# Turning all adjacency rows once, beside layer 0 of the first element, in a four-layer graph kernel

## The chip, the cores and the metric

The kernel runs on one core of a Trainium2 chip. The metric is the device time of one execution in microseconds (us), and the median of several runs is quoted. The engines are called by the names of the profile: PE is the matrix engine (TensorE), PEld its loading of weights, DVE the vector engine, ACT the scalar engine, POOL GpSimd, and SP the engine whose queue issues this kernel's transfers. SBUF is the on-chip working memory, PSUM the memory that PE writes to, DRAM the chip's main memory.

## The reference

There are B = 16 graphs, called elements here, of N = 1024 nodes with D = 64 features each, and an adjacency matrix of 1024 x 1024 zeros and ones per element. Four residual layers follow each other. Before each of them the features are normalised over their 64 values and cut at zero.

```python
# layer 0: thinned adjacency, weighted quantiles over each node's neighbours, two-layer network
h = jnp.maximum(_layernorm(x, axis=-1), 0.0)
x = x + _L0_gnn_ref(h, adj, nodemask, L0_gnn_W1, L0_gnn_b1, L0_gnn_W2, L0_gnn_b2)
# layer 1
h = jnp.maximum(_layernorm(x, axis=-1), 0.0)
A = adj + jnp.eye(N)                                   # _L1_gnn_ref(h, adj)
x = x + jnp.einsum('bij,bjd->bid', A, h) / jnp.sum(A, axis=2, keepdims=True)   # nan -> 0
# layer 2: attention with eight heads, adjacency as a bias on the scores
h = jnp.maximum(_layernorm(x, axis=-1), 0.0)
gamma = jnp.exp(h @ W_gamma.T + b_gamma)
attn = softmax(gamma[..., 0] * q @ k.T * D ** -0.5 + gamma[..., 1] * adj)
x = x + (attn @ v) @ W_proj.T + b_proj
# layer 3
h = jnp.maximum(_layernorm(x, axis=-1), 0.0)
x = x + jnp.einsum('bij,bjo->bio', adj, h @ weight) + bias
```

Layers 1 and 3 both multiply the adjacency matrix by a 1024 x 64 matrix. The matrix engine contracts over partitions, so it wants the columns of the adjacency matrix on the partitions, and the rows must be turned (transposed) first.

## The kernel before

Each element is worked in blocks of 128 nodes: C = 8 blocks, P = 128 partitions, and NH = 2 halves of 512 columns.

**Layer 0** is the largest part. `picks()` (L779) walks through 16 x 8 x 2 x 6 steps of element, feature group, half and quantile. One step is called a comparison: three large DVE operations (`le`, `wa`, `wb` at L819, L821, L823), sums on PE (`prep` and `val`, L842), copies of these on ACT (`wi`, `vs`), a bit test on DVE (L857), a sum on PE (L862) and a product on DVE (L869). An element has 96 of them. `group()` (L713) makes the tables for these comparisons on PE and ACT. `background()` (L967) runs beside them and prepares the next element: it ranks the features of a pair of elements (`ranks`, DVE and transfers of masks `md`) and thins the next adjacency matrix (`dilate`, L470, which reads adjacency rows too). `stages()` (L1016) prepares the next element's neighbour masks near the end of an element, and `leave()` (L1052) runs the small network at its end and gives the element to `done`.

**Layers 1 to 3** of an element are a generator, `rest()` (L1253). In layer 1 (L1089) each block of 128 rows is loaded (`adj_rows`, L465), passed over by ACT in place with an accumulator that gives the row's sum (L1097), turned by `chunk_cols` (L450: eight PE transposes into two PSUM tiles and two ACT copies into `aT`), stored turned to DRAM (`adjT_d`, L1099), and used in `weighted` (L1073: matrix products, a copy, a small product). Layer 3 (L1229) loads the turned blocks back (L1244) and uses `weighted` again. Layer 2 (L1112) loads the rows once for each of four pairs of heads, forms scores on PE, adds the bias and takes the row's extremum on DVE (L1199), exponentiates on ACT, turns the result by `chunk_cols` (`eT`), and multiplies by the values (L1213).

**What sets the order.** The two generators are woven together by a credit, at the end of the program:

```python
    two, due = layers(), 0.0
    for r in picks():
        due += r
        while due > 0.0:
            due -= next(two) or due
```

Each comparison credits 0.42 units. The `yield` values in the layers are their prices: 0.5 + 8 x 0.3 + 0.2 for layer 1, 0.7 + 4 x (0.5 + 8 x 1.0) for layer 2, 0.5 + 8 x 0.3 for layer 3. While the layers wait for an element that layer 0 has not finished, they yield None and the credit is dropped. When all comparisons are done, `alone` is set and the rest of the layers runs by itself with more buffers. Within this program order a scheduler fixes the order of the instructions on each engine when the kernel is built, and every engine then works through its own in that order.

**Buffers and queues.** Adjacency rows use a ring of three buffers (tag `adj`) for layers 1 and 2 and for thinning. Turned blocks use a ring of two (tag `bt`), shared by `aT` and layer 2's `eT`; once `alone` is set, `chunk_cols` has six buffers of another tag. All transfers are issued on SP's queue, one after the other; a transfer that waits for its buffer or its data holds those behind it.

Of the kernel before, what the change touches and what calls it, by code (L numbers as in the profile page):

```python
# [8 lines left out]
F32 = mybir.dt.float32  # L9
# [6 lines left out]
AF = mybir.ActivationFunctionType  # L16
OP = mybir.AluOpType
# [4 lines left out]
P = 128  # L22
# [16 lines left out]
def tile_preln_adj_stack(  # L39
# [30 lines left out]
    nc = tc.nc  # L70
    B, N, D = x.shape
    C = N // P
# [7 lines left out]
    dram = ctx.enter_context(tc.tile_pool(name="dram", bufs=2, space=DRAM))  # L80
# [6 lines left out]
    def tb(name, shape, dt):  # L87
        return sb.tile(list(shape), dt, tag="tb", bufs=6, name=name)
# [5 lines left out]
    def b2_(name, shape=(P, 512), dt=F32):  # L94
        return sb.tile(list(shape), dt, tag="b2", bufs=6, name=name)
# [16 lines left out]
    def pb(name, shape=(P, 512), dt=F32):  # L112
        if alone and name != "pcols":
            return pa(name, shape, dt)
        return ps.tile(list(shape), dt, tag="pb", bufs=2, name=name)

    def small(name, shape, dt=F32, bufs=3):
        return sb.tile(list(shape), dt, tag="s_" + name, bufs=bufs, name=name)
# [271 lines left out]
    sb = ctx.enter_context(tc.tile_pool(name="sb", bufs=1))  # L390
# [11 lines left out]
    def bc(ap, shape):  # L402
        return ap.to_broadcast(list(shape))

    def act(out_, in_, func=AF.Copy, **kw):
        nc.scalar.activation(out_, in_, func, **kw)  # L406

    def adjoining(made):

        first = next(made)  # L410
        with tc.issue_after(first.ins), tc.high_priority():
            for _ in made:
                pass


    def norm_relu(xr, h, t2):

        sh = [P, C, D]
        mean = small("mean", [P, C])
        nc.vector.tensor_reduce(mean, xr, AX.X, OP.add)  # L420
        nc.vector.tensor_scalar(mean, mean, 1.0 / D, None, op0=OP.mult)
        d = t2("d", (P, C, D))
        nc.vector.tensor_tensor(d, xr, bc(mean[:, :, None], sh), OP.subtract)
        sq = t2("sq", (P, C, D))
        act(sq, d, AF.Square)
        ve = small("ve", [P, C])
        nc.vector.tensor_reduce(ve, sq, AX.X, OP.add)
        nc.vector.tensor_scalar(ve, ve, 1.0 / D, EPS, op0=OP.mult, op1=OP.add)
        sd = small("sd", [P, C])
        act(sd, ve, AF.Sqrt)  # L430
        r = small("r", [P, C])
        nc.vector.reciprocal(r, sd)

        e = small("e", [P, C])
        nc.vector.tensor_tensor(e, r, r, OP.mult)
        nc.vector.tensor_tensor(e, e, ve, OP.mult)
        nc.vector.tensor_scalar(e, e, -0.5, 1.5, op0=OP.mult, op1=OP.add)
        nc.vector.tensor_tensor(r, r, e, OP.mult)
        nc.vector.scalar_tensor_tensor(h, d, 0.0, bc(r[:, :, None], sh), op0=OP.max, op1=OP.mult)

    def to_cols(h, hT, rows):

        n = h.shape[2]
        for s in range(NH):
            pt = pb("pt", (n, 4, P))
            for c in range(4):
                nc.tensor.transpose(pt[:, c, :], h[:, 4 * s + c, :], identf)
            nc.scalar.copy(hT[rows, s * 512 : (s + 1) * 512], pt[rows].rearrange("d c p -> d (c p)"))

    def chunk_cols(ad, name):  # L450

        aT = (
            tb(name, (P, C, P), F32) if alone
            else sb.tile([P, C, P], F32, tag="bt", bufs=2, name=name)
        )
        for s in range(2):
            pt = pb("pcols", (P, 4, P))
            adjoining(
                nc.tensor.transpose(pt[:, c, :], ad[:, (4 * s + c) * P : (4 * s + c + 1) * P], identf)  # L459
                for c in range(4)  # L460
            )
            nc.scalar.copy(aT[:, 4 * s : 4 * s + 4, :], pt)  # L462
        return aT

    def adj_rows(b, c):  # L465
        ad = sb.tile([P, N], F32, tag="adj", bufs=3, name="ad")
        nc.sync.dma_start(ad, adj[b, c * P : (c + 1) * P, :])
        return ad
# [604 lines left out]
    def weighted(aT, h):  # L1073

        two = pb("two", (P, P))
        adjoining(
            nc.tensor.matmul(  # L1077
                two[j % 2 * D : j % 2 * D + D, :], h[:, j, :], aT[:, j, :], start=j < 2,
                stop=j >= C - 2, tile_position=(0, j % 2 * D), skip_group_check=True,
            )  # L1080
            for j in range(C)
        )
        part = small("aoT", [P, P], bufs=2)
        nc.scalar.copy(part, two)
        po = pb("po", (P, D))
        nc.tensor.matmul(po, part, ident2, start=True, stop=True)
        return po

    def layer1(b, xr, adjT_d):  # L1089
        h = b2_("h1", (P, C, D))  # L1090
        norm_relu(xr, h, b2_)
        yield 0.5
        o = sb.tile([P, C, D], F32, tag="po", bufs=1, name="o1")
        rc = small("rc1", [P, C], bufs=2)
        for i in range(C):
            ad = adj_rows(b, i)
            act(ad, ad, AF.Copy, accum_out=rc[:, i : i + 1])  # L1097
            aT = chunk_cols(ad, "aT1")
            nc.sync.dma_start(adjT_d[i], aT)  # L1099
            nc.scalar.copy(o[:, i, :], weighted(aT, h))  # L1100
            yield 0.3
        nc.vector.tensor_scalar(rc, rc, 1.0, None, op0=OP.add)
        nc.vector.reciprocal(rc, rc)
        nc.vector.tensor_tensor(o, o, h, OP.add)
        nc.vector.tensor_tensor(o, o, bc(rc[:, :, None], [P, C, D]), OP.mult)
        bad = b2_("bad", (P, C, D), I32)
        nc.vector.tensor_tensor(bad, o, o, OP.not_equal)
        nc.vector.copy_predicated(o, bad, bc(none[:, :, None], [P, C, D]))
        nc.vector.tensor_tensor(xr, xr, o, OP.add)
        yield 0.2  # L1110
# [115 lines left out]
                yield 0.3  # L1226
        residual(*late.pop())

    def layer3(b, xr, adjT_d):  # L1229
        h = b2_("h3", (P, C, D))  # L1230
        norm_relu(xr, h, b2_)
        hT = sb.tile([P, N], F32, tag="hT2", bufs=1, name="h3T")
        to_cols(h, hT, slice(0, D))
        ph = pb("ph3", (P, C, D))
        for j in range(C):
            nc.tensor.matmul(ph[:, j, :], hT[:D, j * P : (j + 1) * P], w3, start=True, stop=True)
        hid = b2_("hid3", (P, C, D))
        nc.scalar.copy(hid, ph)
        nc.vector.tensor_tensor(xr, xr, bc(b3r[:, None, :], [P, C, D]), OP.add)
        yield 0.5  # L1240
        o = sb.tile([P, C, D], F32, tag="po", bufs=1, name="o3")
        for i in range(C):
            aT = sb.tile([P, C, P], F32, tag="bt", bufs=2, name="aT3")
            nc.sync.dma_start(aT, adjT_d[i])  # L1244
            nc.scalar.copy(o[:, i, :], weighted(aT, hid))
            yield 0.3
        nc.vector.tensor_tensor(xr, xr, o, OP.add)
        nc.sync.dma_start(out[b].rearrange("(c p) d -> p c d", p=P), xr)
# [3 lines left out]

    def rest(b):  # L1253
        xr = done.pop(b)
        adjT_d = dram.tile([C, P, C, P], F32, name="adjT_d")
        yield from layer1(b, xr, adjT_d)
        yield from layer2(b, xr)
        yield from layer3(b, xr, adjT_d)

    def layers():  # L1260
        for b in range(B):
            while b not in done:
                yield None
            yield from rest(b)
# [5 lines that stand above are left out]
# [39 lines left out]
```

## Time and profile before

| | |
|---|---|
| median of 3 runs | 12679.28 us (12668.32 to 12680.48) |
| the profiled execution's own time | 12671.61 us |
| its span, first to last instruction | 12669.8 us |
| PE, DVE, ACT busy | 11341.0, 11563.5, 9468.7 us |
| granted PE clock, mean | 0.981 |
| bytes read and written in DRAM | 616.27 MB, 206.57 MB |
| transfers on SP's queue, share of the 16 DMA engines | 19.7% |

A busy time is the union of the recorded instructions of an engine. PE's records are pipelined, so it can be called busy without being at its peak. A window gives the same numbers for a stretch of the span. In a group's name, `out<-in` are the program's tile names with their digits left out, so that `c` stands for both `c0` and `c1`. A wait is put down to the instruction that ended it.

Most of the span is periodic. The first comparison starts at 346.2 us and the ninety-seventh, the first of element 1, at 979.7 us. From there on each element takes between 739 and 784 us up to element 13, 721 us for element 14 and 675 us for element 15, for which no further element has to be prepared. The last comparison starts at 12237.0 us.

### The profile page before, as it was taken

What the parts mean: (1) busy time and instruction counts of PE and PEld (TensorE: products, weight loads), DVE (VectorE), ACT (ScalarE), POOL (GpSimd) and SP (SyncE); (2) the same over time, 40 slices, a digit from 0 to 9 for tenths busy, and PEclk for the clock granted to TensorE, in tenths of its full rate; (3) what the DMA queues carried; (4) which work ended last, traced back from release to release, by engine and by line L of the source; (5) the groups of instructions that cost most, each with busy time, mean ns of one, the idle gap of its engine ahead of it and who ended that gap; (6) DMA issues with size and microseconds to landing.
All of it is one profiled execution on the core that took longest, in us unless ns stands there. A gap on an engine that the chain in (4) does not pass through costs nothing. (4 is left out here: it accounts for less than half of the span.)

```text
span 12669.8 us, 216982 instructions
## 1 busy us (share of the span) xinstructions
PE 11341.0 (90%) x84671; PEld 5347.0 (42%) x84673; DVE 11563.5 (91%) x19682; ACT 9468.7 (75%) x17028; POOL 1.3 (0%) x10
## 2 busy tenths in 40 slices
PE   0779999989899998999989999899998999999998
PEld 0224444444444444444444444444444444444445
DVE  8999989999898998999999999999999999988863
ACT  0557777778777777777877788777887877888866
POOL 0000000000000000000000000000000000000000
PEclk9999999999999999999999999999999999999999
DMA  3012121221212212121121212212121121302121
GB/s 105 28 41 70 52 87 53 66 78 59 83 54 72 73 55 83 53 91 57 57 83 53 94 56 67 76 61 85 56 90 52 64 84 56 99 30 66 34 72 60
DMA packets 503175, 841.07 MB, mean 66 GB/s; under 512 B 238720, under 2 KB 273664, under 8 KB 502144
## 3 DMA queue, kind: packets, MB, share of 16 engines
q1 hardware_dynamic: 502144, 827.20, 19.7%
q8 instruction: 662, 10.85, 0.3%
q14 instruction: 369, 3.02, 0.1%
HBM read 616.27 MB, written 206.57 MB: 65 GB/s over the span
## 5 line engine op out<-in xcount | busy, mean ns | idle before, releaser
L821 DVE TENSOR_TENSOR wa<-le,c 128x2048 f16<-128x2048 f16 x1536 | 1868.2, 1216 | 206.8 <-PE prep L842 173.6
L735 PE MATMUL px<-valid,cw 128*128 128x512 fp8e4 x8192 | 1979.9, 382 | 0.0
L819 DVE TENSOR_TENSOR le<-cum,krow 128x2048 f16<-128x2048 int16 x1536 | 1863.4, 1213 | 12.3 <-PE val L842 10.2
L823 DVE TENSOR_TENSOR wb<-le,c 128x2048 f16<-128x2048 f16 x1536 | 1866.8, 1215 | 1.2 <-PE prep L842 1.2
L406 ACT ACTIVATE c<-px,shifts 128x512 f16<-128x512 f32 x2048 | 1415.3, 698 | 278.9 <-PE px L756 139.0
L406 ACT ACTIVATE s<-s,nm 128x1024 f32<-128x1024 f32 x1024 | 1172.6, 1148 | 188.2 <-DVE nm L1199 184.6
L735 PEld LDWEIGHTS <-cw 128*128 128x128 f16 x8192 | 802.5, 98 | 1113.6 <-issue 231.2
L459 PE MATMUL pcols<-identf,s 128*128 128x128 f32 x8192 | 1168.9, 280 | 94.6 <-ACT eT L462 44.3
L1190 PE MATMUL sp<-kT,qT 64*128 64x512 f32 x4096 | 1166.2, 643 | 61.9 <-DVE nm L1199 59.4
L849 ACT COPY wi<-prep 128x512 f32<-128x512 f32 x1536 | 910.7, 593 | 373.1 <-PE prep L842 301.9
L842 PE MATMUL val<-le,tab 128*32 128x512 f16 x12288 | 1154.6, 386 | 18.1 <-DVE vs L869 7.3
L406 ACT ACTIVATE high<-px,shifts 128x512 f16<-128x512 f32 x1024 | 710.6, 694 | 602.5 <-PE px L735 599.3
L459 PEld LDWEIGHTS pcols<-identf,s 128*128 128x128 f32 x8192 | 900.2, 141 | 617.0 <-ACT eT L462 273.7
L869 DVE SCALAR_TENSOR_TENSOR vs<-pz,vs 128x512 f32<-128x512 f32 x1536 | 1046.6, 681 | 113.7 <-PE pz L862 110.7
L462 ACT COPY eT<-pcols 128x512 f32<-128x512 f32 x2048 | 1134.4, 604 | 20.8 <-PE pcols L459 18.1
L1213 PE MATMUL ao<-eT,v 128*64 128x128 f32 x16384 | 1080.2, 276 | 17.9 <-ACT eT L462 14.0
L406 ACT ACTIVATE vs<-val 128x512 f32<-128x512 f32 x1536 | 938.0, 611 | 161.5 <-PE val L842 108.2
L1213 PEld LDWEIGHTS ao<-eT,v 128*64 128x64 f32 x16384 | 907.5, 137 | 294.6 <-ACT eT L462 135.0
L1199 DVE CUSTOM_DVE_ANT_0 s<-sp,ad,nm 128x512 f32<-128x512 f32 x1024 | 725.9, 744 | 137.8 <-PE sp L1190 137.3
L857 DVE TENSOR_SCALAR bit<-wi,to 128x512 int32<-128x512 int32 x1536 | 826.3, 538 | 2.2 <-ACT cw L406 2.2
L842 PE MATMUL prep<-wb,sel_w 128*32 128x512 f16 x6144 | 650.4, 394 | 189.2 <-DVE wb L823 183.1
L1199 DVE CUSTOM_DVE_ANT_0 s<-sp,ad 128x512 f32<-128x512 f32 x1024 | 681.2, 682 | 128.8 <-PE sp L1190 104.8
(271 smaller groups left out, 18238.8 us busy)
## 6 DMA issues: line engine op xcount, KB each, us to landing
ad<-in_adj_dram SPq DMA_DIRECT2D x768, 512.0 KB
adjT_d<-aT SPq DMA_DIRECT2D x128, 512.0 KB
aT<-adjT_d SPq DMA_DIRECT2D x128, 512.0 KB
md<-sm SPq DMA_DIRECT2D x216, 256.0 KB
sb<-md SPq DMA_DIRECT2D x216, 256.0 KB
rem_d<-rem SPq DMA_DIRECT2D x128, 256.0 KB
left_d<-nb SPq DMA_DIRECT2D x128, 256.0 KB
lr<-left_d SPq DMA_DIRECT2D x256, 128.0 KB
```

The source lines that it names most:

```text
L406: nc.scalar.activation(out_, in_, func, **kw)
L459: nc.tensor.transpose(pt[:, c, :], ad[:, (4 * s + c) * P : (4 * s + c + 1) * P], identf)
L462: nc.scalar.copy(aT[:, 4 * s : 4 * s + 4, :], pt)
L735: yield nc.tensor.matmul(px[pp], w[:, j, :], valid[:, j, :], start=False, stop=j == C - 1, skip_group_check=True,)
L819: nc.vector.tensor_tensor(le, cum, bc(el.krow[q][:, None, hs], [P, 4, 512]), OP.is_lt)
L821: nc.vector.tensor_tensor(wa, le, c0, OP.mult)
L823: last = nc.vector.tensor_tensor(wb, le, c1, OP.mult)
L842: yield nc.tensor.matmul(dst[32 * pp : 32 * pp + 32, :], w[pp], r[pp], start=i == 2, stop=i in (1, 3), tile_position=(0, 32 * pp), skip_gr ...
L869: nc.vector.scalar_tensor_tensor(vs, pz, 80.0, vs, op0=OP.is_equal, op1=OP.mult)
L1190: nc.tensor.matmul(sps[e], qT[e * D : (e + 1) * D, i * P : (i + 1) * P], kT[e * D : (e + 1) * D, hs], start=True, stop=True,)
L1199: nc.vector.tensor_tensor_reduce(ss[e][:, hs], sps[e], ad[:, hs], -1.0, 3.0e38 if t == 0 else nms[e], op0=OP.add, op1=OP.min, accum_out=nm,)
L1213: nc.tensor.matmul(ao[e * D : (e + 1) * D, :], v[:, j, e * D : (e + 1) * D], eTs[e][:, j, :], start=j == 0, stop=j == C - 1, tile_position ...
```

## The change

A new generator, `turned()`, runs ahead of all layers. It goes through the 128 row blocks of all 16 elements: it loads a block, passes over it on ACT with the accumulator (the sums go to one tile, `degree`), turns it and stores it to one of sixteen DRAM tensors, `adjT`, one for each element. Each block has the price 0.3, so the 128 of them cost 38.4 units of the 40.32 that element 0's comparisons credit. Layer 1 no longer loads, sums or turns rows: it loads the turned blocks by `turned_rows()`, as layer 3 did and does, and each of its blocks has the price 0.25 in place of 0.3. The row sums come from `degree`.

```diff
-    def layer1(b, xr, adjT_d):
+    def turned():
+        for b in range(B):
+            for i in range(C):
+                ad = adj_rows(b, i)
+                act(ad, ad, AF.Copy, accum_out=degree[:, b * C + i : b * C + i + 1])
+                nc.sync.dma_start(adjT[b][i], chunk_cols(ad, "aT1"))
+                yield 0.3
+
+    def turned_rows(b, i, name):
+        aT = sb.tile([P, C, P], F32, tag="bt", bufs=2, name=name)
+        nc.sync.dma_start(aT, adjT[b][i])
+        return aT
+
+    def layer1(b, xr):
         h = b2_("h1", (P, C, D))
         norm_relu(xr, h, b2_)
         yield 0.5
         o = sb.tile([P, C, D], F32, tag="po", bufs=1, name="o1")
+        for i in range(C):
+            nc.scalar.copy(o[:, i, :], weighted(turned_rows(b, i, "aT1"), h))
+            yield 0.25
         rc = small("rc1", [P, C], bufs=2)
-        for i in range(C):
-            ad = adj_rows(b, i)
-            act(ad, ad, AF.Copy, accum_out=rc[:, i : i + 1])
-            aT = chunk_cols(ad, "aT1")
-            nc.sync.dma_start(adjT_d[i], aT)
-            nc.scalar.copy(o[:, i, :], weighted(aT, h))
-            yield 0.3
-        nc.vector.tensor_scalar(rc, rc, 1.0, None, op0=OP.add)
+        nc.vector.tensor_scalar(rc, degree[:, b * C : (b + 1) * C], 1.0, None, op0=OP.add)
...
         for i in range(C):
-            aT = sb.tile([P, C, P], F32, tag="bt", bufs=2, name="aT3")
-            nc.sync.dma_start(aT, adjT_d[i])
-            nc.scalar.copy(o[:, i, :], weighted(aT, hid))
+            nc.scalar.copy(o[:, i, :], weighted(turned_rows(b, i, "aT3"), hid))
             yield 0.3
...
-        adjT_d = dram.tile([C, P, C, P], F32, name="adjT_d")
...
+    adjT = [dram.tile([C, P, C, P], F32, name=f"adjT{b}", bufs=1) for b in range(B)]
+    degree = sb.tile([P, B * C], F32, tag="degree", bufs=1, name="degree")
 
     def layers():
+        yield from turned()
         for b in range(B):
             while b not in done:
                 yield None
             yield from rest(b)
```

More of the change, by code (lines that the diff above doesn't have):

```diff
@@ L1227, in layer2, with layer3 @@
         residual(*late.pop())
-    def layer3(b, xr, adjT_d):
+    def layer3(b, xr):
         h = b2_("h3", (P, C, D))
@@ L1254, in rest @@
         xr = done.pop(b)
-        adjT_d = dram.tile([C, P, C, P], F32, name="adjT_d")
-        yield from layer1(b, xr, adjT_d)
+        yield from layer1(b, xr)
         yield from layer2(b, xr)
-        yield from layer3(b, xr, adjT_d)
+        yield from layer3(b, xr)
+    adjT = [dram.tile([C, P, C, P], F32, name=f"adjT{b}", bufs=1) for b in range(B)]
+    degree = sb.tile([P, B * C], F32, tag="degree", bufs=1, name="degree")
     def layers():
+        yield from turned()
         for b in range(B):
```

## The prediction

> **What bounds the kernel now.** I read the page first: the engines' totals, then the costliest groups. The chain that ended last covers only the final part of the span (13% of it), so after that I worked from windows.
>
> ```profile
> PE 11341.0 (90%) x84671; PEld 5347.0 (42%) x84673; DVE 11563.5 (91%) x19682; ACT 9468.7 (75%) x17028; POOL 1.3 (0%) x10
> ```
>
> Two engines are near full and ACT has a quarter free. The order of the comparisons (L819, 96 to an element) cuts the span into stages: start-up to 346 us, element 0's comparisons to 980, fifteen mixed stretches (layer 0 of one element beside layers 1 to 3 of the element before), and a tail from 12237, the last comparison. The windows (columns: stretch, length, busy of PE, PEld, DVE, ACT, POOL, granted clock, DMA share, GB/s) for element 0, an early, a late and the last mixed stretch:
>
> ```profile
> 346.10:979.70 633.60, 504.42 (x2882) 154.78 (x2882) 615.00 (x844) 367.23 (x605) 0.00 (x0) 0.94 0.11 36
> 4806.90:5590.90 784.00, 720.47 (x5301) 335.17 (x5300) 735.56 (x1202) 593.98 (x1067) 0.00 (x0) 0.98 0.20 67
> 9339.20:10099.40 760.20, 698.01 (x5294) 330.70 (x5293) 736.77 (x1205) 590.06 (x1065) 0.00 (x0) 0.99 0.21 71
> 11562.10:12237.00 674.90, 650.48 (x5043) 307.73 (x5041) 575.18 (x876) 541.20 (x990) 0.00 (x0) 1.00 0.14 46
> ```
>
> Element 0 is bound by DVE (615 of 634) and ACT idles 266 us: this is where the change puts work. Stretches 1 to 13 are bound by DVE with PE close behind; the last two by PE (650 of 675). The same work took 784 us early and 760 late. The boundary, 12 comparisons before a new element to 24 after, holds the difference: elements 2, 6, 12 and 13:
>
> ```profile
> 1636.70:1951.90 315.20, 282.07 (x2139) 136.98 (x2140) 273.64 (x450) 237.67 (x441) 0.00 (x0) 0.96 0.26 83
> 4709.00:5027.00 318.00, 283.42 (x2133) 137.42 (x2133) 276.61 (x455) 236.76 (x440) 0.00 (x0) 0.96 0.26 82
> 9238.20:9540.20 302.00, 277.74 (x2139) 135.14 (x2137) 275.96 (x455) 242.79 (x449) 0.00 (x0) 0.98 0.27 87
> 10002.90:10288.70 285.80, 268.40 (x2095) 131.84 (x2091) 262.57 (x445) 230.30 (x429) 0.00 (x0) 0.99 0.29 93
> ```
>
> DVE idles 41 us at an early boundary and 23 to 26 at a late one; elsewhere it idles about 1 us in 12 comparisons. What drifts between early and late is the lag of the layers: one element's layers cost 40.7 units (3.1 + 34.7 + 2.9) and its 96 comparisons credit 96 x 0.42 = 40.32, so the layers fall 0.38 units further back each time, and layer 3 and layer 1 slide off the boundary. Layer 1 itself, from first to last weighted sum of element 4:
>
> ```profile
> 4119.60:4158.90 39.30, 37.55 (x337) 20.83 (x333) 35.63 (x54) 30.21 (x64) 0.00 (x0) 1.00 0.59 198
> ```
>
> PE is at 96% here and DVE still at 91%. The tail, with layer 1 of element 15 in its second line, layer 2 in the third, layer 3 in the last:
>
> ```profile
> 12237.00:12268.00 31.00, 29.03 (x240) 16.45 (x240) 21.43 (x50) 24.90 (x47) 0.00 (x0) 1.00 0.20 70
> 12268.00:12345.00 77.00, 58.99 (x478) 47.73 (x474) 14.96 (x37) 31.22 (x81) 0.00 (x0) 0.73 0.52 181
> 12345.00:12637.00 292.00, 257.34 (x1992) 169.34 (x1992) 111.87 (x315) 207.72 (x388) 0.00 (x0) 0.94 0.16 53
> 12637.00:12669.80 32.80, 24.50 (x161) 20.09 (x160) 0.69 (x1) 4.98 (x18) 0.00 (x0) 0.50 0.31 104
> ```
>
> **What the Trainium skill says.** "Perfetto Trace Analysis", section "Identifying the Most-Contended Engine", warns that matmul occupancy misleads because matmuls are pipelined. The trace agrees: one L735 matmul shows 382 ns, yet 8192 of them cover 1979.9 us, 242 ns each. So I price PE by cover. The same page, "Optimizing Scalar/DVE Operations", says that a profiled latency holds a write acknowledgement that overlaps with the next instruction. Again it agrees: back-to-back L462 copies show 587 ns but start 477 ns apart. "DMA: Bandwidth & Descriptors", section "Anatomy of one DMA", gives about 2.0 us fixed plus bytes over 436 GB/s, an estimate of 3.2 us for 512 KB; in the chain of waits such loads show 3.9 to 5.5 us, and the trace decides.
>
> **The change part by part.**
>
> *One turned row* costs PE eight transposes. The pcols group covers 1168.9 us with 8192, so 8 take 1.14 us. It costs ACT one 1024-wide activation (starts 0.96 apart), its accumulator read (0.09) and two copies (0.48 each): 2.0 us. SP issues a load and a store (0.33 us each). DVE does nothing.
>
> *Element 0.* The built kernel issues the 128 rows evenly: the first five ahead of the first comparison's copies (three of their activations in start-up, where ACT is idle), the last at 89 to 91. ACT gets 123 x 2.0 = 246 us; layer 0 there sums to 345 by starts, so 591 of 634, 93%. PE gets 128 x 1.14 = 146 beside a busy time of 504 that is inflated by pipelining. SP gets 256 issues, 84 us, and DMA another 128 MB, 212 GB/s; layer 1 of the kernel before ran at 188 to 204 GB/s. Lower end 0: everything fits under DVE. Upper end +97: layer 1 turned its rows 5.7 us apart (seven intervals in about 40 us) while 128 in 634 us asks for 4.95, and 128 x 5.7 = 730. Each of the three adjacency buffers is held through a load (4 us), ACT's queue and the transposes, and thinning borrows one of them. Behind a store that waits for its copies SP holds the ranking's mask stores, the thinned rows and the eight-row results of layer 0; DVE and the next element's layer 0 wait for those, with two to six buffers of slack. In the last 24 comparisons ACT's own sums (68 and 76 us) meet stretches of 74 and 68, so it binds there. I take **+40**.
>
> *Layer 1, elements 0 to 14.* Removed per element: 9.1 us of PE, 16 of ACT, one load and one store per row. Added: one load per row from DRAM, through two buffers. Layer 3 reads the same way already: SP waited 265.7 us in all for those buffers, but PE waited only 11.7 us in 16 cases for the landed rows. Behind the waiting load SP holds the next adjacency loads of layer 2 and layer 0's results. The load and store saved give that time back, so I price it at 0 (cover: layer 0's work; without it, 8 landings of about 4 us per element). Each layer 1 is also 0.4 units cheaper (8 x 0.05): layers cost 40.3 against 40.32 credited, so the lag is gone. Every stretch then carries 0.38 units more; the groups L459, L1190 and L1213 cover 3415 us for 512 units, 6.7 us a unit, so 2.5 us of PE and 1 of DVE.
>
> The two effects meet at the boundary. No lag means early boundaries throughout: 41 us of idle DVE instead of the mean 33, +8. Against that, layer 1 was bound by PE and by its transpose-copy-sum chain: 9 us (PE alone) to 25 (PE and ACT in series) go. I take 13. Net -5 in each of 13 stretches: **-65**, from -220 (25 and no loss) to +100 (no relief). Stretches 14 and 15 are bound by PE: 9.1 - 2.5 less, but a worse boundary; **-6** together.
>
> *Tail.* 15 x 0.38 = 5.7 units of element 14 stood behind the last comparison; they move forward. Layer 1 of element 15 then runs alone: about 8 us of norm, eight rows 3.0 us apart (as layer 3's: 12641.35, 12644.36, 12647.38), five DVE operations of 0.7. That is 37 us where 77 stand: **-40**, between -30 and -50. The rest stays.
>
> *Edits at nothing:* degrees kept in one tile (512 bytes per partition), sixteen named DRAM tiles.
>
> Sum: 40 - 65 - 6 - 40 = -71. The profiled execution took 12671.6 us (span 12669.8), so 12600; the median of the runs is 7.7 higher, so about **12610**.
>
> **The rivals.**
>
> *Hidden anyway.* DVE bounds stretches 1 to 13 and did no turning, so relief of PE and ACT only cancels the lost lag: 40 - 40 = 0, 12680. For it: DVE at 94% and more. Against it: PE at 96% inside layer 1.
>
> *Boundaries stay early (slower).* The 41 us come from dependencies at the element's end (its last sums, its output network, the ranking of the next pair), not from transposes. Then +8 x 12 = 96 stays and nothing is relieved: 40 + 96 - 40 = +96, 12775. It decides once relief per boundary is under about 6 us. For it: the idle time fell as the lag grew, with the same turning. Against it: PE idles only 35 of 318 us there.
>
> *Rows pace the opening.* Three buffers and ACT's order set 5.7 us a row: +97 in place of +40, -14 in all, 12665.
>
> *It doesn't do what it says* is excluded: the issue order has all 128 rows within element 0 and no transposes of adjacency afterwards.
>
> **How the numbers follow.** Forecast 0.56 (own range 12540 to 12650), hidden 0.15, early boundaries 0.20, rows pace 0.09. A measurement of this kernel tells about 0.2%, 25 us, from no change. Faster by more: the forecast, 0.56. Within: hidden and half of the rows' case, 0.20. Slower: early boundaries and the other half, 0.24. The range that leaves out no more than 2 in 10 goes from 12540, under which only the largest relief lies, to 12755, into the early-boundary case.
>
> **What would show it.** Element 0's comparisons should take 660 to 690 us with ACT above 85%; over 720 means that the rows pace it. DVE's idle time at a boundary should be about 28 to 36 us at elements 2 and 12 alike; 41 or more is the slower rival. The tail after the last comparison should be 385 to 400 us. ACT's copies waiting for adjT stores, or PE for aT loads, by more than 50 us in all would mean a queue cost that I set at nothing. The forecast is wrong if opening and boundaries together lose more than the tail's 40 us gives.

## The result, and the profile after

The changed kernel takes 12621.25 us (median of six runs, 12614.32 to 12624.76) against 12681.68 for the kernel before (six runs, 12668.32 to 12688.10): a ratio of 0.9955, 95% interval 0.9943 to 0.9966. That is 60 us faster by the medians and 0.45% by the ratio; 12610 had been forecast. The profiled execution took 12620.06 us with a span of 12618.3, and all parts below are parts of this span.

The engines' totals hardly show the change: the span lost 51.5 us, PE 70 us of busy time, ACT 3.

```profile
PE 11271.0 (89%) x84666; PEld 5355.3 (42%) x84673; DVE 11557.3 (92%) x19682; ACT 9465.7 (75%) x17018; POOL 1.4 (0%) x10
```

The same windows as before, cut at the same comparisons: element 0, an early, a late and the last mixed stretch (columns as before: stretch, length, busy of PE, PEld, DVE, ACT, POOL, granted clock, DMA share, GB/s).

```profile
349.10:1007.80 658.70, 564.50 (x3887) 256.37 (x3887) 615.40 (x845) 599.83 (x1097) 0.00 (x0) 0.98 0.69 237
4767.50:5541.40 773.90, 704.93 (x5235) 329.68 (x5235) 731.38 (x1194) 577.47 (x1034) 0.00 (x0) 0.98 0.20 64
9307.30:10081.10 773.80, 704.77 (x5235) 329.65 (x5235) 731.41 (x1194) 577.41 (x1034) 0.00 (x0) 0.98 0.20 64
11543.20:12232.60 689.40, 648.33 (x5010) 303.06 (x5008) 579.97 (x886) 528.58 (x960) 0.00 (x0) 0.98 0.12 38
```

Element 0 takes 25 us longer (633.6 before) with the same DVE work; ACT went from 367 to 600 us busy, and the transfers from 36 to 237 GB/s. The early and the late stretch are now alike to the microsecond: where 784 and 760 stood there are 773.9 and 773.8. The last stretch is longer than before, 689 against 675, although PE has a little less to do in it.

The boundaries before elements 2, 6, 12 and 13 (12 comparisons before the element's first to 24 after):

```profile
1642.70:1955.30 312.60, 280.41 (x2100) 135.71 (x2100) 276.33 (x457) 227.21 (x419) 0.00 (x0) 0.96 0.23 70
4668.30:4979.30 311.00, 279.53 (x2100) 134.84 (x2100) 276.25 (x457) 227.36 (x419) 0.00 (x0) 0.96 0.23 71
9208.20:9519.10 310.90, 279.33 (x2100) 134.80 (x2100) 276.29 (x458) 227.34 (x419) 0.00 (x0) 0.96 0.23 71
9989.20:10279.40 290.20, 264.69 (x2016) 127.96 (x2016) 261.10 (x445) 216.86 (x399) 0.00 (x0) 0.97 0.26 79
```

DVE idles 36, 35, 35 and 29 us (length less DVE's busy time). No drift is left; what is left is a period of two elements, about 35 us at even ones and 28 at odd ones. The tail after the last comparison: the first line ends with the last addition of element 15's output network (`leave()`), the second with the last DVE operation of its layer 1, and the last is layer 3.

```profile
12232.60:12259.90 27.30, 20.07 (x168) 11.18 (x164) 10.95 (x16) 6.67 (x19) 0.00 (x0) 0.88 0.45 130
12259.90:12293.30 33.40, 20.82 (x144) 16.60 (x144) 7.53 (x17) 4.65 (x18) 0.00 (x0) 0.50 0.41 126
12293.30:12586.00 292.70, 256.76 (x1994) 169.58 (x1995) 111.96 (x316) 207.95 (x389) 0.00 (x0) 0.94 0.16 53
12586.00:12618.30 32.30, 24.10 (x160) 19.69 (x159) 0.69 (x1) 4.69 (x18) 0.00 (x0) 0.50 0.33 106
```

Cut at the same operations, the kernel before takes 31.5, 76.4, 292.1 and 32.8 us: 43 of the tail's 47 us lie in the stretch that ends with layer 1.

By parts the account of the two profiled executions reads as follows.

| part, us | before | after | difference |
|---|---|---|---|
| start-up, to the first comparison | 346.2 | 349.1 | +2.9 |
| element 0's comparisons | 633.5 | 658.7 | +25.2 |
| stretches 1 to 13 | 9861.7 | 9812.6 | -49.1 |
| stretches 14 and 15 | 1395.6 | 1412.1 | +16.5 |
| tail | 432.8 | 385.6 | -47.2 |
| sum | 12669.8 | 12618.1 | -51.7 |

(Each part is rounded; the spans differ by 51.5.)

Opening, stretches 1 to 13 and tail have the sign of the forecast and roughly its size (25 for 40, 49 for 65 and 47 for 40 us); stretches 14 and 15 have the other sign. The experiments ask whether they have its reasons as well.

### The profile page after: what moved, and what is told of

Its sections match the earlier page's. It is cut to its first block, busy times and chain, and to the rows that moved or that the text cites. A ratio compares the mean times of both kernels' runs of the same rounds, so it can differ in the third digit from the quotient of the medians.

```text
span 12618.3 us, 217315 instructions
## 1 busy us (share of the span) xinstructions
PE 11271.0 (89%) x84666; PEld 5355.3 (42%) x84673; DVE 11557.3 (92%) x19682; ACT 9465.7 (75%) x17018; POOL 1.4 (0%) x10
## 3 DMA queue, kind: packets, MB, share of 16 engines
q1 hardware_dynamic: 520576, 894.31, 21.9%
## 5 line engine op out<-in xcount | busy, mean ns | idle before, releaser
L459 PE MATMUL pcols<-identf,s 128*128 128x128 f32 x8192 | 1177.8, 281 | 112.5 <-ACT eT L462 49.1
L869 DVE SCALAR_TENSOR_TENSOR vs<-pz,vs 128x512 f32<-128x512 f32 x1536 | 1047.2, 682 | 148.4 <-PE pz L862 110.4
```

The source lines that it names most:

```text
L869: nc.vector.scalar_tensor_tensor(vs, pz, 80.0, vs, op0=OP.is_equal, op1=OP.mult)
```

## The experiments

The ratios in this section are to the kernel before, run on the same chip beside each kernel. "Parts" are the five rows of the table above, and the opening is the second of them. They come from one profiled execution of each kernel. As a measure of chance: the changed kernel and two later edits that act only in the tail take 9812.6, 9809.5 and 9815.5 us in stretches 1 to 13, and 658.7 to 660.4 in the opening.

**The price alone.** Two things in the change act on stretches and tail: turning leaves layer 1, and layer 1's price falls so that the layers no longer fall back. First the price without the turning, on the kernel before.

```diff
             nc.scalar.copy(o[:, i, :], weighted(aT, h))
-            yield 0.3
+            yield 0.25
```

> The kernel before with one edit: a row of layer 1 is priced 0.25 in place of 0.3, so the layers cost 40.3 units against 40.32 credited and never lag, while layer 1 still turns its own rows. Theory (two effects meet at an element's boundary: no lag makes every boundary an early one, and the removed turning is what gives that back): all boundaries of elements 2 to 13 show 41 to 44 us of idle DVE, stretches 1 to 13 lose about 50 to 100 us, stretches 14 and 15 lose about 17, the tail gains 25 to 30 (the 5.7 units move forward, the turning in the tail stays): 12720 to 12770, slower. Rival (the lower price, not the turning, made the kernel faster): the mixed stretches take what they take in the changed kernel, and with the shorter tail the time is 12600 to 12640.

It took 12672.74 us, ratio 0.9998 (0.9990 to 1.0006): neither theory's number. The parts explain it: stretches 1 to 13 took 9878.3 us (+16.6), stretches 14 and 15 1431.3 (+35.7), the tail 379.7 (-53.1). The 5.7 units that stood behind the last comparison did move forward, and the stretches took back in full what the tail gave. The tail is even 6 us shorter than in the changed kernel, though layer 1 of element 15 still turns its rows in it (its stretch, cut as above, takes 26.9 us against 33.4). So the tail's 47 us were the moved units; taking the turning out of the tail gained nothing there. The loss in the stretches is smaller than the +8 a boundary that I had counted: 16.6 us in 13. The boundaries show why (elements 6 and 7 of this kernel):

```profile
4668.30:4990.00 321.70, 284.69 (x2166) 140.76 (x2169) 276.49 (x460) 241.20 (x446) 0.00 (x0) 0.95 0.26 82
5459.30:5749.70 290.40, 267.16 (x2077) 129.13 (x2076) 262.21 (x447) 229.67 (x426) 0.00 (x0) 0.99 0.29 91
```

Length less DVE's busy time is 45 and 28 us, and again 45 and 27 at elements 12 and 13. Without lag, the even boundaries stay at 45 and the odd ones, 43 at elements 3 and 5 of the kernel before, are at 28. "No lag means early boundaries throughout" was wrong for every second one.

**The turning alone, with the old price.** The other half: the changed kernel with layer 1's rows at 0.3, so that the lag grows as before.

```diff
             nc.scalar.copy(o[:, i, :], weighted(turned_rows(b, i, "aT1"), h))
-            yield 0.25
+            yield 0.3
```

> The changed kernel with layer 1's rows priced 0.3 as before, so the layers fall 0.38 units further behind with each element, as they did, but without the turning. Theory: opening +25 as in the changed kernel; the boundaries get better with the lag as they did before and keep the relief of the turning, so idle DVE falls from about 35 to 20 us between elements 2 and 13 and stretches 1 to 13 gain 80 to 150 us on the kernel before; the tail gives back the moved 5.7 units and gains only the turning, 10 to 20 us: 12540 to 12610, faster than the changed kernel. Rival (the lag does nothing, only the turning counts): mixed stretches as in the changed kernel and a longer tail: 12640 to 12660.

12663.08 us, ratio 0.9990 (0.9982 to 0.9999). Its parts: 660.2 in the opening, 9841.8 in stretches 1 to 13, 1381.6 in 14 and 15, 432.5 in the tail, where the stretch of layer 1 takes 75.8 us, close to the 76.4 of the kernel before, with no row turned in it. Stretches 1 to 15 gain 34 us and the opening takes most of them back. Neither half alone is worth more than 0.1%: with the 28 us of start-up and opening set aside, turning alone gives 34, the price alone nothing, both together about 80. With the lag gone, removing the turning is worth 66 us in stretches 1 to 13 and 19 in 14 and 15; with the lag growing it is worth 20 and 14.

**Turning without use.** The kernel before with `turned()` ahead of its layers, and layer 1 as it was, prices the opening by itself.

```diff
     def layers():
+        yield from turned()
         for b in range(B):
```

> The kernel before with all 128 rows turned in addition beside element 0's comparisons, into DRAM tensors that nothing reads; layer 1 still turns its own rows at 0.3. It isolates the price of the opening. Theory: the opening's comparisons grow by 25 us as in the changed kernel (658.7 against 633.5) and everything after is as in the kernel before: 12695 to 12715. Rival (the opening's growth in the changed kernel was an accident of another order and the rows are hidden): 12670 to 12690. Rival (rows pace the opening at 5.7 us each): 12770 or more.

12719.39 us, ratio 1.0040 (1.0027 to 1.0053), and the opening takes 665.7 us, +32; in the changed kernel it is +25. Stretches and tail together are 14 us above the kernel before; no later instruction uses what was turned, and I have no reason for these 14.

**What of the opening costs.** I had named ACT at 93% as the reason for +40, and the rows' own pace as a rival. Three edits of the changed kernel, each of `turned()`. First without ACT's pass (the row sums are left out, and layer 1 divides by a constant):

```diff
                 ad = adj_rows(b, i)
-                act(ad, ad, AF.Copy, accum_out=degree[:, b * C + i : b * C + i + 1])
...
+    nc.vector.memset(degree, 1.0)
```

> The changed kernel without ACT's pass over the rows in the opening: the row sums are left out and layer 1 divides by a constant. It takes about 1.05 us of ACT from each turned row, 128 to 134 us in all, and leaves loads, transposes, copies and stores. Theory (ACT, at 600 of 659 us, makes the opening grow): the opening falls back to about 640 us and the whole to 12595 to 12610. Rival (PE, the three adjacency buffers or the transfers make it grow): opening unchanged within 5 us, 12615 to 12625.

12618.00 us, ratio 0.9955 (0.9942 to 0.9967), the same as the changed kernel. ACT's busy time in the opening fell by 111 us, and the opening did not shorten; it grew from 658.7 to 669.2:

```profile
345.80:1015.00 669.20, 574.44 (x3889) 265.90 (x3889) 614.01 (x836) 488.49 (x851) 0.00 (x0) 0.95 0.67 233
```

So taking ACT's pass away gained nothing in sum. The waits of that window say what stands there (single lines of the list: waiting engine and line, what ended the wait, us in all, times, longest):

```profile
PE pcols L459 <- DMA ad<-in_adj_dram: 26.8, 16, 4.0
...
DVE vs L869 <- PE pz L862: 21.8, 17, 6.1
DVE wa L821 <- PE prep L842: 21.2, 16, 2.8
```

The same window of the changed kernel:

```profile
ACT ad L406 <- DMA ad<-in_adj_dram: 19.9, 23, 2.3
...
PE pcols L459 <- ACT ad L406: 16.2, 15, 2.2
DVE vs L869 <- PE pz L862: 15.8, 13, 1.9
...
DVE wa L821 <- PE prep L842: 6.8, 6, 2.4
```

With the pass, ACT meets a late row; without it PE does, in order, and layer 0's sums wait behind the transposes. ACT's copies also waited 21.9 us for stores of turned rows, against 2.7 in the changed kernel. The loss is DVE's idle time in both, 55.2 and 43.3 us where the kernel before has 18.6; the two waits of DVE shown are most of the increase without the pass, and less than half of it with the pass (they are 8.0 and 4.0 us in the kernel before). That reading of the two lists is argued, since the edit changed two things at once: ACT's load, and which engine first touches a row.

The second edit leaves ACT's pass and takes the eight transposes and two copies away (the rows are stored as they were loaded, so that layers 1 and 3 sum over the wrong index):

```diff
-                nc.sync.dma_start(adjT[b][i], chunk_cols(ad, "aT1"))
+                nc.sync.dma_start(adjT[b][i], ad.rearrange("p (c q) -> p c q", c=C))
```

> The changed kernel with the turning left out of the opening: rows are loaded, summed by ACT and stored as they are, so layers 1 and 3 multiply by wrong blocks; 1024 transposes and 256 copies of the opening are gone, every transfer stays. Theory, changed after the run without row sums, in which the opening grew by 36 us though ACT was 112 us less busy: the growth comes from the transposes and copies that stand in order between layer 0's own instructions on PE and ACT. Then the opening falls to 635 to 645 us. Rival (the transfers, SP's queue and the ring of three adjacency buffers): opening 655 to 670.

12606.88 us, ratio 0.9950 (0.9936 to 0.9963); the opening takes 643.1:

```profile
349.10:992.20 643.10, 518.31 (x2882) 154.87 (x2882) 616.29 (x844) 467.36 (x804) 0.00 (x0) 0.91 0.58 202
```

Without transposes and copies the opening gets back about 16 of its 25 us; the other 10 stay with transfers and ACT's pass. The place of the loss tells more. The last 24 comparisons of element 0, where the forecast had seen ACT bind, in the kernel before, the changed kernel, the one without the pass and the one without transposes and copies:

```profile
838.20:979.70 141.50, 120.75 (x787) 41.98 (x787) 137.60 (x179) 95.73 (x163) 0.00 (x0) 0.99 0.19 53
851.50:1007.80 156.30, 137.59 (x990) 62.23 (x990) 137.66 (x180) 142.93 (x264) 0.00 (x0) 1.00 0.69 226
857.00:1015.00 158.00, 143.27 (x998) 64.56 (x997) 135.10 (x171) 120.61 (x215) 0.00 (x0) 0.97 0.67 224
846.50:992.20 145.70, 125.24 (x789) 42.82 (x788) 138.31 (x179) 108.76 (x190) 0.00 (x0) 0.95 0.46 154
```

Of the 25 us 15 lie here. Without the pass ACT is 76% busy in place of 91%, and the time is no shorter; without transposes and copies 11 of the 15 are gone. So the loss here does not need a full ACT. Whether it is PE's transposes or ACT's copies of them was not separated. What the missing pass cost lies elsewhere, in comparisons 49 to 72 (179.7 us against 167.9); over all others the two kernels agree within 2 us.

The third edit lets the rows come faster, at a price of 0.2:

```diff
-                yield 0.3
+                yield 0.2
```

> The changed kernel with a turned row priced 0.2 in place of 0.3, so all 128 rows are due within the first 61 comparisons, 3.2 us a row. It shows how fast rows can go. Theory (a cost of about 0.2 us a row that does not depend on the pace, until ACT is full: 61 comparisons need 216 us of ACT and 128 rows 256, 472 together against 415 to 420 of DVE's): the opening grows by 70 to 110 us over the kernel before, 705 to 745, with ACT over 90% busy in its first 60% and none of it in the rest. Rival (a row cannot go faster than 4.9 to 5.7 us, the buffers' pace): the first 61 comparisons take 627 to 730 us and the opening 850 or more. Rival (DVE's own pace hides them still): 655 to 670.

12665.06 us, ratio 0.9996 (0.9987 to 1.0004). The opening takes 697.2, a little under what was expected, and its first half has both engines short of full:

```profile
348.40:700.00 351.60, 282.38 (x1990) 141.59 (x1990) 308.03 (x430) 332.81 (x619) 0.00 (x0) 0.98 0.83 294
```

The group of the stores of turned rows, in the answer for their tile (shortest, median and longest issue in ns, then first and last start), gives the rows' pace:

```profile
L1096 SPq DMA_DIRECT2D adjT<-aT x128: 319/326/1612, 334.2 to 838.6; - x128
```

127 intervals in 504.4 us are 4.0 us a row, where the changed kernel asks for 4.95; a pace of 5.7 us set by buffers is excluded. In the first half ACT is busy 95% and DVE 88%, and the loss is 64 us in place of 25: crowding the rows is what costs.

**Where the layers stand against the boundary.** If the mixed stretches gain by where layers 1 and 3 fall, a constant lag should move all boundaries together. The changed kernel, set back by 3 units once:

```diff
             while b not in done:
                 yield None
+            if b == 0:
+                yield 3.0
             yield from rest(b)
```

> The changed kernel with one line more: before layer 1 of element 0 the layers let 3.0 units of credit pass, once, so they run 3 units behind in every stretch. The price 0.25 stays, so the lag neither grows nor shrinks. Theory (it is the place of layers 3 and 1 against the element's end that sets the idle time there, and 3 units is a good place: with the old price, elements 8 and 9 had such a lag and 27.5 and 26.4 us of idle DVE against 36.8 and 26.8 in the changed kernel): boundaries 27 us each, stretches 1 to 13 gain 40 to 70 us, stretches 14 and 15 gain 10 to 25, the tail loses about 25 for 3 units: 12560 to 12600. Rival (the difference between places is chance of the order): mixed stretches as in the changed kernel, tail +25: 12640 to 12655.

12622.71 us, ratio 0.9961 (0.9946 to 0.9976). DVE's idle time at boundaries 2 to 13 is 30.7 us in the mean against 31.8, but scattered from 20.9 to 43.5; stretches 1 to 13 gain 6 us and the tail loses 20. The 6 us are no more than the spread by chance. The lag as such does nothing that I could name in advance.

**What of layer 1 relieves the stretches.** On the kernel with the lower price alone, once without ACT's pass in layer 1 (row sums left out, division by a constant), once without its transposes and copies (layers 1 and 3 sum over the wrong index).

```diff
+        nc.vector.memset(rc, 1.0)
...
-            act(ad, ad, AF.Copy, accum_out=rc[:, i : i + 1])
```

> The kernel before with layer 1's rows at 0.25 (no lag, rows still turned inside layer 1), but without ACT's pass over the rows there: the row sums are left out and layer 1 divides by a constant. Theory: what relieves the mixed stretches in the changed kernel is that transposes and their copies are gone, not the pass on ACT, so stretches 1 to 13 stay at 9860 to 9880 us in sum and the total at 12655 to 12675. Rival: ACT's pass is what holds layer 1; then they fall to 9815 to 9840 and the total to 12595 to 12625.

```diff
-            aT = chunk_cols(ad, "aT1")
+            aT = ad.rearrange("p (c q) -> p c q", c=C)
```

> The kernel before with layer 1's rows at 0.25, its eight transposes and two copies per row left out: a row is passed over by ACT, stored and multiplied as it was loaded, so layers 1 and 3 sum over the wrong index. Theory: transposes and copies are the relief; stretches 1 to 13 fall from 9878 to 9815-9835 us in sum, stretches 14 and 15 from 1431 to about 1412, nothing is paid in the opening, total 12590 to 12615. Rival: it is the layer's rows standing ready in DRAM, or one transfer fewer per row, that relieves; then nothing moves, 12655 to 12675.

Without the pass: 12671.71 us, ratio 0.9995 (0.9986 to 1.0003), stretches 1 to 13 at 9871.6. Without transposes and copies: 12597.58 us, ratio 0.9936 (0.9923 to 0.9950), stretches 1 to 13 at 9819.4, 14 and 15 at 1408.7. The theory holds: leaving out transposes and copies gives 59 of the 66 us that the changed kernel gains there over the price alone, and 23 in stretches 14 and 15, where the changed kernel gains 19. The two were taken out together, so how the gain divides between PE's transposes and ACT's copies is not shown.

How this reaches DVE, which turned nothing, can be seen in the waits of stretches 1 to 13, and so can a trap. With the price alone, the first DVE operation that needs layer 1's rows (L1104, once for each element) stands too early in DVE's order and holds everything behind it on DVE:

```profile
DVE o L1104 <- ACT o L1100: 59.0, 12, 8.2
...
DVE wa L821 <- PE prep L842: 37.5, 51, 2.2
```

Those 59 us (4.6 in the kernel before) are nearly the gain, and in the changed kernel the wait (L1115 there) is down to 11.5. But without ACT's pass it is down too, and the time is not:

```profile
DVE wa L821 <- PE prep L842: 131.6, 86, 5.6
...
DVE o L1104 <- ACT o L1100: 19.1, 13, 6.2
```

There 40 us left this wait and 94 turned up at the comparisons' own sums, while DVE's idle time over the 13 stretches went from 557.5 to only 549.0. Without transposes and copies it went to 503.3, in the changed kernel to 494.2. Of the two edits only the one that took the transposes and copies away brought the idle time clearly down.

**Layer 1 alone, in the tail.** The turned rows of element 15 come 3.0 us apart, as predicted. Is that the two buffers, or PE's own chain?

```diff
-        aT = sb.tile([P, C, P], F32, tag="bt", bufs=2, name=name)
+        aT = (
+            tb(name, (P, C, P), F32) if alone
+            else sb.tile([P, C, P], F32, tag="bt", bufs=2, name=name)
+        )
```

> The changed kernel, but once layer 0 is done the turned rows are loaded into the ring of six buffers that the turning itself used there, in place of the ring of two; before that nothing changes. In the kernel with the price alone the eight weighted sums of the last layer 1 stand 1.9 us apart (rows turned ahead while the element's end was worked out); in the changed kernel they stand 3.0 apart. Theory (two buffers and the landing of a load set 3.0 us a row): layer 1 and layer 3 of element 15 take 1.9 us a row, 8 to 9 us less each: the tail 385.6 becomes 366 to 372 and the whole 12600 to 12608. Rival (PE's own chain sets 3.0): tail unchanged, 12615 to 12625.

12623.23 us, ratio 0.9962 (0.9949 to 0.9974), tail 385.8: nothing, the rows still 3.0 us apart. The buffers are not it. In the timeline of PE in the changed kernel (start, duration, engine, line, operation, and the idle time before it with what ended it) a row is a burst of 16, a wait for ACT's copy, a small product, and the next burst:

```profile
12268.24 1.98 PE L1077 MATMUL two<-aT,h 128*64 128x128 f32 x16
12270.58 0.69 PE L1086 MATMUL po<-ident,aoT 128*128 128x64 f32 x2 [0.36 <-ACT aoT L1084]
12271.20 1.98 PE L1077 MATMUL two<-aT,h 128*64 128x128 f32 x16
```

With the price alone, where the rows are still turned between the bursts, the same burst takes 1.09 us from the third row on, and the rows come 1.9 us apart:

```profile
12326.36 1.98 PE L1077 MATMUL two<-aT,h 128*64 128x128 f32 x16
12328.27 0.66 PE L459 MATMUL pcols<-identf,ad 128*128 128x128 f32 x4
...
12329.07 1.09 PE L1077 MATMUL two<-aT,h 128*64 128x128 f32 x16
...
12330.95 1.09 PE L1077 MATMUL two<-aT,h 128*64 128x128 f32 x16
```

More work per row, and the row is faster: there the granted clock rose, from 0.51 (12323.1 to 12328.3) to 1.00 (12329.0 to 12339.5); in the changed kernel it stays at 0.50 (second and last line of its tail). So the last edit closes PE's gaps: once the layers run alone, the next row's burst is issued ahead of the small product of the row before, with six buffers for turned rows.

```diff
+    def weighted_rows(b, h, o, name, price):
+        held = []
+        for i in range(C):
+            held.append((i, partial(turned_rows(b, i, name), h)))
+            while len(held) > (1 if alone and i < C - 1 else 0):
+                k, part = held.pop(0)
+                nc.scalar.copy(o[:, k, :], whole_sum(part))
+            yield price
...
-        for i in range(C):
-            nc.scalar.copy(o[:, i, :], weighted(turned_rows(b, i, "aT1"), h))
-            yield 0.25
+        yield from weighted_rows(b, h, o, "aT1", 0.25)
```

(`partial` and `whole_sum` are `weighted` cut in two behind its copy; layer 3 has the same edit; the burst's tile has a PSUM tag of its own once alone.)

> The changed kernel, with the rows of layers 1 and 3 pipelined once the layers run alone: the sums of the next row stand on PE ahead of the small product of the row before, and turned rows have six buffers. Theory: with PE's chain to ACT and back covered, rows go 1.5 to 2.3 us apart in place of 3.0 and the granted clock rises above its 0.50; layers 1 and 3 of element 15 give 6 to 12 us each, the tail takes 360 to 375 us, the total is 12595 to 12610. Rival: the clock stays at 0.50, the rows go about 2.5 us apart, the tail takes about 378 us and the total 12612 to 12620.

12605.29 us (12602.20 to 12611.89), ratio 0.9941 (0.9929 to 0.9954), the tail 364.4 in place of 385.6; all other parts within 3 us of the changed kernel. Its rows:

```profile
12269.36 3.68 PE L1077 MATMUL two<-aT,h 128*64 128x128 f32 x32 [7.49 <-DVE h L439]
...
12273.48 1.09 PE L1077 MATMUL two<-aT,h 128*64 128x128 f32 x16
12274.50 0.43 PE L1089 MATMUL po<-ident,aoT 128*128 128x64 f32 x2
12274.87 1.09 PE L1077 MATMUL two<-aT,h 128*64 128x128 f32 x16
```

From the third on they are 1.39 us apart. Layer 3's window of rows, at half clock in the changed kernel:

```profile
12583.10:12596.30 13.20, 13.07 (x144) 10.98 (x144) 0.00 (x0) 3.62 (x15) 0.00 (x0) 0.84 0.24 81
```

PE is 99% busy and the clock 0.84. Both layers gain 11 us: layer 1's stretch takes 22.3 us in place of 33.4, layer 3 from its first row on 17.3 in place of 28.3. Of the kernels that leave nothing out this is the fastest, some 16 us ahead of the changed kernel by the medians, which were taken on different chips; the parts of the profiled executions say 18.

## Why the prediction was right

*The time.* 12610 was forecast, 12621 measured, and the sum -71 stands against -52 of the profiled execution. The forecast case came true, in part by luck: two terms were near for the wrong reasons, and one had the wrong sign.

*Element 0, +40.* +25, just under the 660 to 690 us that were to show it, with ACT at 91%. The size was within its bounds and the place right, since 15 of the 25 us lie in the last 24 comparisons; the reason, ACT near full and binding there, was not: at 76% ACT they take as long. Without transposes and copies 16 of the 25 go, and 10 stay with transfers and the pass. Start-up's 3 us were not priced.

*Stretches 1 to 13, -65.* -49. The net was near by luck: two errors cancelled. The lost lag, +8 a boundary, is +1.3 a stretch (16.6 in 13), because only the even boundaries stay early. The +8 was also read too high: DVE's idle time at boundaries 2 to 13 of the kernel before is 34.9 us in the mean, not 33. The relief, -13, is -5.1 (66 in 13). What I had not seen is that the effects depend on each other: the relief is worth 20 us with the lag growing and 66 without. The boundary's idle time, 28 to 36 us at elements 2 and 12 alike, is 36.3 and 34.6. One bound was worked out wrongly: 25 us in 13 boundaries without a loss are -325; -220 is 25 less the loss of 8.

*Stretches 14 and 15, -6.* +16.5, the step that failed. I took PE's work there as the whole price, "9.1 - 2.5 less, but a worse boundary", and put the worse boundary at nearly nothing. The price alone costs 35.7 us, and with it PE idles 87 us in the two stretches against 61 before; the missing turning gives 19 back. Of these 35.7 us 26 lie in three short slices: the first 12 comparisons of each stretch (110.4 and 100.5 us with the price alone, 100.8 and 95.2 before) and the last 12 of stretch 15 (83.4 and 72.0). PE is busy 252 us in these slices in both kernels, so what they lost is PE's waiting, which my pricing by work left out.

*Tail, -40.* -47, at 385.6 (385 to 400 was to show it). The moved units are all of it, -53 by the price alone; "37 us where 77 stand" measured 33.4 where 76.4 stood, and rows at 3.0 us apart, though foreseen, were a loss against 1.9 with transposes between them.

*Queues, nothing.* Right: PE waited for turned rows 14.7 us in 24 cases in the whole run, ACT's copies for the stores of turned rows 2.7 us in the opening, where 50 was the alarm. (The loads of 512 KB of adjacency rows in the chain of waits took 3.8 to 5.5 us; the 3.9 was misread.)

*The rivals.* "Hidden anyway" falls: without transposes and copies the stretches shorten. "Boundaries stay early" had its cause half right, since even boundaries do stay at 45 us where nothing is relieved, but with the relief they are at 35. "Rows pace the opening" is excluded at 4.0 us a row.

*What stays open.* Why only the even boundaries stay early without lag is not settled: features are ranked for pairs of elements, which has the same period, but no run varied it. Which of transfers and ACT's pass holds the opening's 10 us was not separated, nor was it shown what PE waits for in the three slices of stretches 14 and 15.

## What to carry to other kernels

When work is moved to other cover and a price in the schedule changes with it, run the two halves apart: here one half was worth nothing, the other about what the new place cost, and only both together gained. A gain in the tail is none until the stretches have been added up, since units that leave the tail are done somewhere else, and a wait that leaves a list is time only if the engine's idle time falls with it. Where a small chain runs alone, put the next step's matrix work ahead of the wait.

## What the runs showed of the hardware

I had not expected that less work on PE could make a row slower. The burst of 16 products takes 1.98 us at a granted clock of 0.50 and 1.09 at full clock, and in layer 1 of element 15 in the changed kernel PE never leaves half clock, though its records cover 20.82 of the 24.20 us from 12265.2 on, in which the rows run. The Trainium skill describes this in "TensorE: Matmul & The Clock Gate", section "What's actually happening" of Part 1: "the default state is throttled, and activity releases the throttle". The runs agree: there the bursts, with gaps of 0.36 to 0.42 us for ACT's copy, stay at 0.50, and in the last edit the same bursts without gaps are released within 4.1 us (0.50 from the first burst at 12269.36 on, 1.00 from the one at 12273.48 on). With the lower price alone the clock was released as well, with transposes between the bursts (1.98 us for the burst at 12326.36, 1.09 for the next).
